# Front stage of a fused attention and mixture-of-experts kernel: work of the first four tiles spread between weight products, another load order, and bf16 products on TensorE during the first loads

## The chip, the cores and the metric

The kernel runs on one core of one Trainium2 chip. The metric is the device time of one execution in microseconds; the time before is the median of five runs. A profile of one further execution gives, for each engine, when each instruction ran and what it waited for. TensorE is called PE in the profile, its weight loads PEld, VectorE DVE, ScalarE ACT, GpSimd POOL, and SyncE, which here only issues transfers, SP.

## The reference

For hidden states `x` of 2 x 1024 tokens with 512 features, the reference computes a layer norm, single-head attention, a router-weighted mixture of two of eight experts, and a gate:

```python
xn = layernorm(x)                                   # mean and variance over 512, eps 1e-5
qkv = xn @ w_qkv.T + b_qkv                          # q, k, v of 512 each
s = softmax(q @ k.T / sqrt(512)) @ v @ w_out.T + b_out
logits = xn @ router_w + router_b                   # 8 experts, the best two, softmax of the two
h = silu(xn @ expert_w[e] + expert_b[e])            # combined with the two weights
y = xn + combined @ proj_w + proj_b
g = silu(norm_w * y / sqrt(mean(y * y) + 1e-6))
out = x + s * g
```

## The kernel before, in words

The 2048 tokens are 16 tiles of 128 rows. The kernel has a front stage, a stage of products per tile (`pv`), the router, the experts (`ph`), and attention with the projection and the gate. All arithmetic is float32, and the order of instructions on every engine is the order in which the Python code writes them (`keep_order`). A step that waits on an engine therefore holds everything written after it on the same engine. The same is true of the transfers that SP issues.

The change is in the front stage. What follows are its steps, with the names that the profile shows.

The matrices Wv and Wo are multiplied beforehand, so that one product of a tile gives values that already went through the output matrix. `load_wv(c)` brings a quarter of Wv (256 KB), `load_wo(n)` a half of Wo (512 KB), `spread` brings Wq in four transfers of 256 KB into `wZ`, in runs of 512 bytes, and `load_x(t)` brings a tile of `x` (256 KB). The router matrix is 16 KB and goes to columns of the tile `rwvo`, in runs of 32 bytes.

`turn_wv(c)` turns a quarter of Wv: four transpositions on PE against the identity into one bank of PSUM (`wvt`), and a copy by DVE (`wvT`). `product_vo(n, hc)` is one of eight weight products: four matmuls of 256 columns, which the profile lists as eight, since each float32 matmul is two passes, and a copy by ACT into `rwvo` (`pvo`, lines 363 to 374).

`norm(g)` treats two tiles. DVE computes mean and variance (`bnst`, `mv`), ACT a square root (`std`), DVE the reciprocal and the shift (`rstd`, `shift`), and ACT the scaled rows. For the first four tiles (`DIRECT = 4`) ACT makes the rows twice: as `xw`, which PE turns, and as `xn`, with columns in another order, which goes to DRAM for the experts. For the other tiles `xn` goes to DRAM (`put`) and comes back rearranged (`take`), and DVE turns it in blocks. `turn_x(t)` is that last step: for the first four tiles four PE transpositions into a bank (`xt`) and a DVE copy into `xnT`, for the others one DVE transposition of `xz`.

`turn_w` turns Wq on DVE (four instructions at line 134), `weighted` forms the sum `sq` from it on DVE (lines 285 and 287), and `columns` makes of it one column on PE (`pw`), which DVE copies into the router's columns of `rwvo`. `pbb` is a small product for a bias.

The loop over 16 tiles at line 403 then multiplies each turned tile by `rwvo` (`pv`, line 411): 265 columns, the router's nine among them, then 256. ACT copies the values (`vo`), DVE adds the router's bias (`lg`). Two double banks (`ps_big`) serve `pv`; four banks (`ps_mm`) serve all the small products in turn. In the loop, `norm` runs six tiles ahead of `pv`, and `turn_x` two tiles ahead.

Of the kernel before, what the change touches and what calls it, by code (L numbers as in the profile page):

```python
# [10 lines left out]
FP = mybir.dt.float32  # L11
BF = mybir.dt.bfloat16
I32 = mybir.dt.int32
AF = mybir.ActivationFunctionType
# [6 lines left out]
P = 128  # L21
# [6 lines left out]
def kernel(  # L28
# [17 lines left out]
    B, S, H = hidden.shape  # L46
    E = router_w.shape[1]
    KC = H // P
    NTOK = B * S
    NT = NTOK // P  # L50
# [7 lines left out]
    scale = 1.0 / math.sqrt(H)  # L58
# [103 lines left out]
    E1 = E + 1  # L162
# [7 lines left out]
    def load_x(t):  # L170
        x[t] = ln.tile([P, H], FP, tag="x", name=f"x{t}", bufs=8)
        sp.dma_start(x[t], x_d[:, t, :])
# [7 lines left out]
    def load_wv(c):  # L180
        sp.dma_start(wv_in[:, c, :], w_qkvT[ts(c, P), ts(2, H)])

    def load_wo(n):
        sp.dma_start(
            wo[:, :, ts(n, HH)], w_outT[:, ts(n, HH)].rearrange("(c p) h -> p c h", p=P)
        )

    act.dma_start(bqkv, b_qkv.rearrange("p (i c) -> p i c", i=3))
    act.dma_start(rw[:, :, 0:E], router_w.rearrange("(c p) e -> p c e", p=P))
    load_wv(0)  # L190
    load_wo(0)
    for c in range(1, KC):
        load_wv(c)
    for t in range(2):
        load_x(t)
    load_wo(1)
    spread(sp, wZ[0], w_qkvT[:, ts(0, H)])
    for t in range(2, 8):
        load_x(t)

    ident = const.tile([P, P], FP, name="ident")
    make_identity(nc, ident)
# [76 lines left out]
    def weighted(w_, bias, name):  # L279

        s_ = raw.tile([P, H], FP, tag="s", name=name, bufs=3)
        for c in range(KC):
            b_ = bias[:, c : c + 1]
            if c:
                dve.scalar_tensor_tensor(s_, w_[:, c, :], b_, s_, ALU.mult, ALU.add)
            else:
                dve.tensor_scalar(s_, w_[:, c, :], b_, None, ALU.mult)
        return s_

    def columns(s_, name):  # L290

        ps = ps_mm.tile([P, 512], FP, tag="mm", name=name)
        for c in range(KC):
            pe.matmul(
                ps[:, c : c + 1], lhsT=s_[:, ts(c, P)], rhs=ones[:, 0:1], start=True, stop=True
            )
        return ps[:, 0:KC]

    DIRECT = 4

    def norm(g):

        gs = ts(g, 2)
        two = (2 * g, 2 * g + 1)
        for t in two:
# [3 lines left out]
        act.activation(  # L309
            std[:, gs], mv[:, gs, 1:2].rearrange("p t o -> p (t o)"), AF.Sqrt, bias=ln_eps  # L310
        )
        dve.reciprocal(rstd[:, gs], std[:, gs])
        dve.scalar_tensor_tensor(
            shift[:, gs], mv[:, gs, 0:1].rearrange("p t o -> p (t o)"), -1.0, rstd[:, gs],
            ALU.mult, ALU.mult,
        )
        for t in two:
            scaled = dict(bias=shift[:, t : t + 1], scale=rstd[:, t : t + 1])
            if t < DIRECT:
                xw[t] = raw.tile([P, H], FP, tag="xw", name=f"xw{t}", bufs=DIRECT)  # L320
                act.activation(xw[t], x[t], AF.Identity, **scaled)
            xn_[t] = ln.tile([P, H], FP, tag="xn", name=f"xn{t}", bufs=5)
            act.activation(in_turn(xn_[t]), own(x[t]), AF.Identity, **scaled)
        if two[0] >= DIRECT:
            for t in two:
                xs[t] = dram.tile([4, P, P], FP, tag="xn_s", name=f"xn_s{t}", bufs=6)
                put(xs[t], xn_[t])
        for t in two:
            if t + 8 < NT:
                load_x(t + 8)  # L330
        for t in two:
            sp.dma_start(xn_d[ts(t, P), :], xn_[t])
        if two[0] >= DIRECT:
            for t in two:
                xz[t] = ln.tile([P, 4, P], FP, tag="xz", name=f"xz{t}", bufs=6)
                take(xz[t], xs.pop(t))

    xs, xz, xn_, xw = {}, {}, {}, {}

    def turn_x(t):  # L340
        dst = xnT[t // ST][:, :, ts(t % ST, P)]
        if t >= DIRECT:
            turn(dst, xz.pop(t))
            return
        ps = ps_mm.tile([P, 512], FP, tag="mm", name=f"xt{t}").rearrange(
            "p (j f) -> p j f", j=KC
        )
        for j in range(KC):
            pe.transpose(ps[:, j, :], xw[t][:, ts(j, P)], ident)
        dve.tensor_copy(dst, ps)  # L350
# [3 lines left out]
    def turn_wv(c):  # L354
        ps = ps_mm.tile([P, 512], FP, tag="mm", name=f"wvt{c}").rearrange(
            "p (o f) -> p o f", o=KC
        )
        for oc in range(KC):
            pe.transpose(ps[:, oc, :], wv_in[:, c, ts(oc, P)], ident)
        wvT[c] = raw.tile([P, KC, P], FP, name=f"wvT{c}")  # L360
        dve.tensor_copy(wvT[c], ps)

    def product_vo(n, hc):
        at_, size = halves[n]
        ps = ps_mm.tile([P, 512], FP, tag="mm", name=f"pvo{hc}_{n}")
        for c in range(KC):
            pe.matmul(
                ps[:, :size],
                lhsT=wvT[hc][:, c, :],
                rhs=wo[:, c, ts(n, HH)],  # L370
                start=(c == 0),
                stop=(c == KC - 1),
            )
        act.copy(rwvo[:, hc, at_ : at_ + size], ps[:, :size])
# [21 lines left out]
    pe.matmul(pbb[:, 0:KC], lhsT=ones, rhs=bb, start=True, stop=True)  # L396
    dve.tensor_reduce(rb[:, E:E1], pbb[:, 0:KC], AX.X, ALU.add)
    turn_x(0)
    turn_x(1)
    dve.tensor_copy(rw[:, :, E], columns(sq_, "pw"))  # L400


    for t in range(NT):
        if t % 2 == 0 and t + 6 < NT:
            norm(t // 2 + 3)
        if t + 2 < NT:
            turn_x(t + 2)
        pv = ps_big.tile([P, 2, 512], FP, tag="big", name=f"pv{t}")
        for n, cols in enumerate((ds(0, HH + E1), ds(HH + E1, HH))):
            for c in range(KC):  # L410
                pe.matmul(  # L411
                    pv[:, n, : HH + E1 * (1 - n)],
                    lhsT=xnT[t // ST][:, c, ts(t % ST, P)],
                    rhs=rwvo[:, c, cols],
                    start=(c == 0),
                    stop=(c == KC - 1),
                )
        dst = vo[t // ST][:, t % ST, :].rearrange("p (n f) -> p n f", n=2)
        act.copy(dst, pv[:, :, 0:HH])
        dve.tensor_tensor(lg1[:, t, :], pv[:, 0, HH : HH + E1], rb, ALU.add)  # L420
        if t == 1:
            spread(sp, wZ[1], w_qkvT[:, ts(1, H)])
        if t == 2:
            gps.dma_start(bo, b_out.partition_broadcast(P))
        if t == 4:
            turn_w(wqkT[:, KC:], wZ[1])
        if t == 6:
            sk_ = weighted(wqkT[:, KC:], bqk[:, 0], "sk")
        if t == 8:

            vb = weighted(wo, bqkv[:, 2], "vb")
        if t == 9:
            dve.tensor_copy(u, columns(sk_, "pu"))
        if t == 11:
            pvb = ps_mm.tile([P, 512], FP, tag="mm", name="pvb")
            pe.matmul(pvb, lhsT=ones, rhs=vb, start=True, stop=True)
            dve.tensor_tensor(bo, pvb, bo, ALU.add)
            close(raw_guard)
            ew_guard, ewp = pool("ew", side="right")
            ew = ewp.tile([P, E, KC, H], FP, name="ew")  # L440
        if t == 12:
            for e in range(E):
                sp.dma_start(ew[:, e], expert_w[e].rearrange("(c p) f -> p c f", p=P))
# [762 lines left out]
```

## Time and profile before

| | us |
|---|---|
| median of five runs | 558.38 |
| lowest and highest run | 552.31, 561.65 |
| all five | 552.75, 559.30, 561.65, 558.38, 552.31 |
| the profiled execution's own time | 554.18 |
| span from its first to its last instruction | 552.3 |
| PE busy, share of the span | 529.1, 96% |
| DVE busy, share | 314.5, 57% |
| ACT busy, share | 160.6, 29% |
| mean granted clock of PE | 0.986 |

The profiled execution took 554.18 us, of which 552.3 us lie between the first and the last instruction. The median of the runs is 4.20 us above it. A busy PE is not PE at its peak: a row for matmuls with the clock at half speed is as busy as one at full speed. The view of 40 slices therefore has a line of its own for the clock that PE was granted.

### The profile page before, as it was taken

Reading aid. Unit: us, or ns where it says so; the run is one execution under the profiler, and the core shown is the slowest. Engines: PE = TensorE matmul, PEld = TensorE weight load, DVE = VectorE, ACT = ScalarE, POOL = GpSimd, SP = SyncE. Lnnn points to the kernel's source line nnn. Section 1 sums busy time; section 2 is a strip of 40 time slices with the busy share of each in tenths; the row PEclk is TensorE's granted clock in tenths of the full one; section 3 lists DMA queues with packets and bytes.
Section 4 is the critical chain, followed back from the end, with each engine's and each line's share of the span. In section 5 each row is a group of like instructions: output and inputs, shape, how many; then the busy total and the mean of one; then the engine's idle time right before and its main releaser. Section 6 shows DMA issues by size and latency. Waiting matters only on the chain.

```text
span 552.3 us, 5745 instructions
## 1 busy us (share of the span) xinstructions
PE 529.1 (96%) x1736; PEld 323.4 (59%) x1736; DVE 314.5 (57%) x522; ACT 160.6 (29%) x262; POOL 224.8 (41%) x230
## 2 busy tenths in 40 slices
PE   5899999999999999999997999999999999999985
PEld 4788887444444444443545666756746556474855
DVE  1836763821333333343788257375798685948655
ACT  1634312111211111111323422423325243242413
POOL 5000000023245763220678536238837575646070
PEclk9979999999999999999997999999999999999999
DMA  9899569738899999989476913715416656282702
GB/s 249 257 328 270 178 201 381 290 98 262 262 279 329 301 313 293 290 248 278 157 223 205 331 54 110 271 39 193 188 38 183 237 162 256 88 293 78 266 31 83
DMA packets 90783, 118.65 MB, mean 215 GB/s; under 512 B 6912, under 2 KB 54912, under 8 KB 90624
## 3 DMA queue, kind: packets, MB, share of 16 engines
q1 hardware_dynamic: 78672, 89.15, 50.7%
q0 software_dynamic: 5792, 18.88, 10.9%
q10 hardware_dynamic: 6288, 10.25, 5.0%
q8 instruction: 14, 0.23, 0.2%
q14 instruction: 17, 0.14, 0.1%
HBM read 73.69 MB, written 44.56 MB: 214 GB/s over the span
## 4 chain that ended last, share of the span: by engine, by line
PE 63%; DMA 22%; DVE 7%; issue 5%; SPq 1%; ACT 1%; POOL 1%; ACTq 0%; DVEq 0%; POOLq 0%
PE so L1018 13%; PE pp L953 13%; PE pv L411 11%; PE po L891 10%; DMA xs<-xg 7%; DMA xg<-xn_d,tok 7%; PE pq L454 5%; PE pr L473 4%; PE ph L712 3%; PE pqk L485 2%; PE sc L934 1%; DMA ho_d<-h 1%; DMA sz<-xs 1%; DMA x<-_attn_hidden_states_dram 1%; DMA pz<-ps 1%
## 5 line engine op out<-in xcount | busy, mean ns | idle before, releaser
L712 PE MATMUL ph<-ew,gT 128*128 x280 | 120.6, 593 | 1.2 <-DVE gT L120 1.2
L686 POOL DMA_INDIRECT xg<-xn_d,tok x39 | 37.4, 959 | 183.2 <-DVE npast L632 103.9
L712 PEld LDWEIGHTS ph<-ew,gT 128*128 128x128 f32 x280 | 53.0, 190 | 68.6 <-issue 66.0
L738 DVE TENSOR_TENSOR h<-ph,eb 128x512 f32<-128x512 f32 x39 | 26.7, 687 | 74.3 <-issue 42.9
L411 PE MATMUL pv<-rwvo,xnT 128*128 128x265 f32 (+1 forms) x256 | 59.0, 391 | 0.0
L891 PE MATMUL po<-pw,ct 128*128 128x512 f32 x128 | 56.3, 593 | 2.1 <-DVE ct L120 2.1
L411 PEld LDWEIGHTS pv<-rwvo,xnT 128*128 128x128 f32 x256 | 49.3, 194 | 9.2 <-issue 0.5
L741 ACT ACTIVATE h<-h 128x512 f32<-128x512 f32 x39 | 24.6, 630 | 102.6 <-DVE h L738 82.4
L1025 DVE TENSOR_TENSOR o<-so,o 128x256 f32<-128x256 f32 (+1 forms) x57 | 22.9, 415 | 42.9 <-PE so L1018 21.4
L891 PEld LDWEIGHTS po<-pw,ct 128*128 128x128 f32 x128 | 24.2, 190 | 31.3 <-issue 31.2
L953 PE MATMUL pp<-xnT,qT 128*128 128x512 f32 x84 | 39.6, 593 | 0.4 <-DVE o L1025 0.4
L1052 POOL TENSOR_TENSOR o<-o,base 128x512 f32<-128x512 f32 x14 | 20.2, 1462 | 46.2 <-DVE o L1043 46.2
L1018 PE MATMUL so<-vo,pT 128*128 128x256 f32 x168 | 38.5, 379 | 0.0
L853 POOL DMA_INDIRECT hg<-ho_d,posi_m x32 | 30.9, 967 | 18.2 <-DMA cs<-hg 9.9
L120 DVE STREAM_TRANSPOSE gT<-sz 128x512 f32<-128x512 f32 x39 | 27.5, 705 | 19.0 <-DMA sz<-xs 18.9
L1018 PEld LDWEIGHTS so<-vo,pT 128*128 128x128 f32 x168 | 31.9, 190 | 7.3 <-issue 3.1
L921 ACT ACTIVATE pr<-sc,nm 128x1024 f32<-128x1024 f32 x16 | 18.3, 1142 | 60.3 <-DVE nm L918 60.3
L959 DVE TENSOR_TENSOR sc<-pp,sc 128x512 f32<-128x512 f32 x49 | 31.7, 682 | 6.6 <-PE pp L953 6.4
L473 PE MATMUL pr<-xnT,wqk 128*128 128x256 f32 x128 | 31.6, 408 | 3.0 <-DVE sc L959 3.0
L473 PEld LDWEIGHTS pr<-xnT,wqk 128*128 128x128 f32 x128 | 26.4, 207 | 9.3 <-DVE sc L959 3.4
L120 DVE STREAM_TRANSPOSE pT<-pz 128x1024 f32<-128x1024 f32 x14 | 28.3, 2019 | 0.0
L454 PE MATMUL pq<-xnT,wqk 128*128 128x512 f32 x64 | 28.1, 594 | 0.0
(198 smaller groups left out, 768.4 us busy)
## 6 DMA issues: line engine op xcount, KB each, us to landing
xs<-xg SPq DMA_DIRECT2D x39, 256.0 KB
sz<-xs SPq DMA_DIRECT2D x39, 256.0 KB
ho_d<-h ACTq DMA_DIRECT2D x39, 256.0 KB
ew<-in_L_ffn_expert_w_dram SPq DMA_DIRECT2D x8, 1024.0 KB
ps<-pr SPq DMA_DIRECT2D x16, 512.0 KB
pz<-ps SPq DMA_DIRECT2D x16, 512.0 KB
x<-_attn_hidden_states_dram SPq DMA_DIRECT2D x16, 256.0 KB
xn_d<-xn SPq DMA_DIRECT2D x16, 256.0 KB
```

What stands on the lines that cost most here:

```text
L120: dve.transpose(dst.rearrange(f"p j {order} -> p i j a", a=QP), z.rearrange("p i (j b) -> p i j b", b=QP),)
L411: pe.matmul(pv[:, n, : HH + E1 * (1 - n)], lhsT=xnT[t // ST][:, c, ts(t % ST, P)], rhs=rwvo[:, c, cols], start=(c == 0), stop=(c == KC - 1),)
L454: pe.matmul(ps[:, half, :], lhsT=wqk[:, c, ts(oc, P)], rhs=xnT[0][:, c, ts(half, 512)], start=(c == 0), stop=(c == KC - 1),)
L473: pe.matmul(ps[:, :PW], lhsT=wqk[:, c, ts(oc, P)], rhs=xnT[1][:, c, ts(k, PW)], start=(c == 0), stop=(c == KC - 1),)
L686: gps.indirect_dma_start(out=xg[s], out_offset=None, in_=xn_d, in_offset=bass.IndirectOffsetOnAxis(ap=tok[:, s : s + 1], axis=0),)
L712: pe.matmul(ph, lhsT=g_[:, c, :], rhs=ew[:, ds(r, 1), c, :].rearrange("p e f -> p (e f)"), start=(c == 0), stop=(c == KC - 1),)
L738: dve.tensor_tensor(h, ph, eb[:, ds(r, 1), :].rearrange("p e f -> p (e f)"), ALU.add)
L853: gps.indirect_dma_start(out=g_, out_offset=None, in_=ho_d, in_offset=bass.IndirectOffsetOnAxis(ap=posi_m[:, n, t : t + 1], axis=0),)
L891: pe.matmul(po, lhsT=c_[:, c, :], rhs=pw[:, c, :], start=(c == 0), stop=(c == KC - 1))
L953: pe.matmul(ps, lhsT=l_[:, c, :], rhs=r_[:, c, :], start=(c == 0), stop=(c == KH - 1))
L959: dve.tensor_tensor(dst, ps, other, ALU.add)
L1018: pe.matmul(ps[:, :w_], lhsT=l_[:, c, :], rhs=r_[:, c, :], start=(c == 0), stop=(c == SK - 1),)
```

## The change

The first transfers go in another order: two quarters of Wv ahead of Wo, four tiles of `x` ahead of the second half of Wo and of Wq, and the router matrix behind Wq on SP's queue, no longer on ACT's. A bf16 tile of ones is set by POOL ahead of the identity, and `hold(n)` issues n bf16 products of 256 columns into a bank that nobody reads: 12 ahead of `turn_wv(0)` and 6 ahead of `turn_wv(1)`.

`norm` is cut into `stats`, `shifts`, `direct` and `rows`, and for the first four tiles these pieces are written between the weight products. `turn_x(0)` and `turn_x(1)` stand ahead of `pbb`, the third group of `norm` stands behind the copy of `pw`, and `turn_x(2)` is the first step of the loop. In `pv` the 256 columns that hold no router column come first.

```diff
     act.dma_start(bqkv, b_qkv.rearrange("p (i c) -> p i c", i=3))
-    act.dma_start(rw[:, :, 0:E], router_w.rearrange("(c p) e -> p c e", p=P))
     load_wv(0)
+    load_wv(1)
     load_wo(0)
-    for c in range(1, KC):
+    for c in range(2, KC):
         load_wv(c)
-    for t in range(2):
+    for t in range(4):
         load_x(t)
     load_wo(1)
     spread(sp, wZ[0], w_qkvT[:, ts(0, H)])
-    for t in range(2, 8):
+    sp.dma_start(rw[:, :, 0:E], router_w.rearrange("(c p) e -> p c e", p=P))
+    for t in range(4, 8):
         load_x(t)
+    idle = const.tile([P, 2 * P], BF, name="idle")
+    gps.memset(idle, 1.0)
+
+    def hold(n):
+        ps = ps_mm.tile([P, 512], FP, tag="mm", name="hold")
+        for _ in range(n):
+            pe.matmul(ps[:, : 2 * P], lhsT=idle[:, 0:P], rhs=idle, start=True, stop=True)
...
+    def direct(t):
+        xw[t] = raw.tile([P, H], FP, tag="xw", name=f"xw{t}", bufs=DIRECT)
+        normed(xw[t], x[t], t)
...
+    def norm(g):
+        stats(g)
+        shifts(g)
+        rows(g)
...
+    hold(12)
     turn_wv(0)
+    hold(6)
     turn_wv(1)
-    for hc in range(KC):
-        product_vo(0, hc)
-        if hc + 2 < KC:
-            turn_wv(hc + 2)
-        if hc == 2:
-            norm(0)
+    product_vo(0, 0)
+    turn_wv(2)
+    stats(0)
+    product_vo(0, 1)
+    turn_wv(3)
+    product_vo(0, 2)
+    stats(1)
+    shifts(0)
+    direct(0)
+    product_vo(0, 3)
+    direct(1)
+    shifts(1)
     turn_w(wqkT[:, 0:KC], wZ[0])
     product_vo(1, 0)
-    norm(1)
+    direct(2)
+    direct(3)
 
     bb = raw.tile([P, KC], FP, name="bb")
     dve.tensor_tensor(bb, bqkv[:, 0, :], bqkv[:, 1, :], ALU.mult)
     product_vo(1, 1)
+    rows(0)
     sq_ = weighted(wqkT[:, 0:KC], bqk[:, 1], "sq")
     product_vo(1, 2)
-    norm(2)
+    turn_x(0)
     product_vo(1, 3)
+    rows(1)
+    turn_x(1)
     pbb = ps_mm.tile([P, 512], FP, tag="mm", name="pbb")
     pe.matmul(pbb[:, 0:KC], lhsT=ones, rhs=bb, start=True, stop=True)
     dve.tensor_reduce(rb[:, E:E1], pbb[:, 0:KC], AX.X, ALU.add)
-    turn_x(0)
-    turn_x(1)
     dve.tensor_copy(rw[:, :, E], columns(sq_, "pw"))
+    norm(2)
 
 
     for t in range(NT):
+        if t == 0:
+            turn_x(2)
         if t % 2 == 0 and t + 6 < NT:
             norm(t // 2 + 3)
-        if t + 2 < NT:
+        if 0 < t < NT - 2:
             turn_x(t + 2)
         pv = ps_big.tile([P, 2, 512], FP, tag="big", name=f"pv{t}")
-        for n, cols in enumerate((ds(0, HH + E1), ds(HH + E1, HH))):
+        for n, cols in ((1, ds(HH + E1, HH)), (0, ds(0, HH + E1))):
```

The new `stats`, `shifts` and `rows` hold the lines of the old `norm` unchanged: statistics and square root, reciprocal and shift, and the `xn` rows with their transfers (new loads of `x`, stores to `xn_d`, `put` and `take`).

More of the change, by code (lines that the diff above doesn't have):

```diff
@@ L299, with stats @@
     DIRECT = 4
-    def norm(g):
+    def stats(g):
         gs = ts(g, 2)
-        two = (2 * g, 2 * g + 1)
-        for t in two:
+        for t in (2 * g, 2 * g + 1):
             st = ln.tile([P, 6], FP, tag="bnst", name=f"bnst{t}", bufs=4)
@@ L311, in norm, with shifts @@
         )
+    def shifts(g):
+        gs = ts(g, 2)
         dve.reciprocal(rstd[:, gs], std[:, gs])
@@ L316, in norm, with normed, rows @@
         )
+    def normed(dst, src, t):
+        act.activation(
+            dst, src, AF.Identity, bias=shift[:, t : t + 1], scale=rstd[:, t : t + 1]
+        )
+    def direct(t):
+        xw[t] = raw.tile([P, H], FP, tag="xw", name=f"xw{t}", bufs=DIRECT)
+        normed(xw[t], x[t], t)
+    def rows(g):
+        two = (2 * g, 2 * g + 1)
         for t in two:
[L318 to L321, printed above, removed]
             xn_[t] = ln.tile([P, H], FP, tag="xn", name=f"xn{t}", bufs=5)
-            act.activation(in_turn(xn_[t]), own(x[t]), AF.Identity, **scaled)
+            normed(in_turn(xn_[t]), own(x[t]), t)
         if two[0] >= DIRECT:
```

## The prediction

> **What bounds the kernel now.** I read the page first, then PE by time, then the clock in slices of 1 us, then DVE and ACT over the same stretch, and SP's own waits last.
>
> ```profile
> span 552.3 us, 5745 instructions
> PE 529.1 (96%) x1736; PEld 323.4 (59%) x1736; DVE 314.5 (57%) x522; ACT 160.6 (29%) x262; POOL 224.8 (41%) x230
> ...
> PEclk9979999999999999999997999999999999999999
> ```
>
> PE is busy nearly throughout, so only a stage with holes or with a low clock has time to give. The clock line has two such places: the third slice (27.6 to 41.4 us) and the twenty-second. The change lies ahead of the first. PE's timeline there:
>
> ```profile
> 3.81 1.09 PE L359 MATMUL wvt<-ident,wv_in 128*128 128x128 f32 x4 [3.81 <-DMA wv_in<-in_L_attn_w_qkv_dram]
> 6.87 1.11 PE L359 MATMUL wvt<-ident,wv_in 128*128 128x128 f32 x4 [1.97 <-DMA wv_in<-in_L_attn_w_qkv_dram]
> 7.78 3.35 PE L367 MATMUL pvo<-wo,wvT 128*128 128x256 f32 x8
> ...
> 11.40 1.89 PE L367 MATMUL pvo<-wo,wvT 128*128 128x256 f32 x8
> 13.13 0.60 PE L359 MATMUL wvt<-ident,wv_in 128*128 128x128 f32 x4
> 13.57 10.53 PE L367 MATMUL pvo<-wo,wvT 128*128 128x256 f32 x48
> 23.93 0.28 PE L396 MATMUL pbb<-bb,ones 128*128 128x4 f32 x2
> 26.24 1.09 PE L349 MATMUL xt<-ident,xw 128*128 128x128 f32 x8 [2.03 <-ACT rwvo L374]
> 28.50 1.87 PE L294 MATMUL pw<-ones,sq 128*128 128x1 f32 x8 [1.16 <-DVE rb L397]
> 30.23 1.09 PE L349 MATMUL xt<-ident,xw 128*128 128x128 f32 x4
> 31.11 5.42 PE L411 MATMUL pv<-rwvo,xnT 128*128 128x265 f32 x16
> ```
>
> The weight products end at 24.1 us, but the first `pv` starts only at 31.11. Between them PE does little and waits twice, for ACT and for DVE. From there on `pv` is gapless, and the chain that ended last runs through PE's products down to the experts: what the front saves, the end should save. Eight rows of `pvo` take 10.53/6 = 1.755 us late, but 3.35 the first time: PE runs at half speed there. The 1 us slices show it happening again:
>
> ```profile
> 27.00:28.00 1.00, 0.34 (x4) 0.10 (x1) 0.61 (x2) 0.29 (x1) 0.00 (x0) 0.89 0.67 238
> 28.00:29.00 1.00, 0.50 (x3) 0.50 (x3) 0.96 (x5) 0.59 (x1) 0.00 (x0) 0.50 0.97 367
> ...
> 34.00:35.00 1.00, 1.00 (x4) 0.78 (x4) 0.00 (x0) 0.51 (x1) 0.00 (x0) 0.69 1.07 410
> ```
>
> The clock is the third number from the end. It falls at 27.78 (0.11 of a slice at a loss of 0.5 is 0.22 us) and returns at 34.62. DVE and ACT say what PE waited for:
>
> ```profile
> 18.17 2.49 DVE L134 STREAM_TRANSPOSE qT<-wZ 128x512 f32<-128x512 f32 x4
> ...
> 23.56 2.47 DVE L285 SCALAR_TENSOR_TENSOR sq<-qT,bqk,sq 128x512 f32<-128x512 f32 x3
> ...
> 28.36 1.28 DVE L350 COPY xnT<-xt 128x512 f32<-128x512 f32 x2
> ```
>
> ```profile
> 25.84 0.62 ACT L374 COPY rwvo<-pvo 128x256 f32<-128x256 f32 x2
> ```
>
> ACT copies the last weight products late, behind four `xw`/`xn` rows of 0.8 us, and `xt` waits 2.03 us for that bank. DVE ends `sq` at 26.03, works through the statistics of tiles 4 and 5, and only at 28.36 takes up what lets `pw` go. SP's waits tell when Wq lands:
>
> ```profile
> SPq L172 <- DMA wZ<-in_L_attn_w_qkv_dram: 2.2, 3, 1.1
> ```
>
> These end near 15.6 us. The slices show 180 to 207 GB/s from 11 to 16 us, the 512-byte runs of `wZ`, then 366. So `wZ` has landed by about 16.1, and `turn_w` at 18.17 did not wait for it; it waited behind `std` and `shift`.
>
> **The change, part by part.** First PE alone. The second quarter of Wv landed just before 6.87 with three 256 KB units and the router matrix ahead of it or beside it. Afterwards the same megabyte brings both quarters and half of Wo, so I let the first product start at 6.9 (7.78 before). Eight products by 1.755 are 14.0; `wvt` for the last two quarters and `xt` for two tiles are four by 0.44 (13.13 to 13.57), 1.8; `pbb` 0.3. That ends at 23.0. `pw` at full clock is 0.8 (1.87 here at half, and the same form in the loop at 68.64 lasts 0.79 in the chain) and `xt` for tile 2 is 0.44: `pv` could start at 24.2.
>
> Now DVE, which I think decides. `wZ` has two loads of `x` more ahead of it: 0.52 MB by some 350 GB/s (slices from 6 to 10 us, 313 to 397) is 1.5 us, so it lands at 17.6, less what the router matrix no longer takes (16 KB in 512 runs; nothing to 0.5 us). I take 17.5. All that stands ahead on DVE is done by then: `stats(0)` 10.0 to 11.8, the last `wvT`, `stats(1)` 12.5 to 14.2 by 1.69 a pair (14.38 to 16.07), the shifts by 15. Then `turn_w` 2.41 (18.17 to 20.58), `bb` and `sq` 3.07 (22.88 to 25.95), one copy of `xnT` 0.64: 23.6. The copy also frees `pw`'s bank. `pw` 0.8 and `xt` 0.44 give 24.85, later than PE's own 24.2. I take 24.9 for the first `pv`, against 31.11: 6.2 us.
>
> The second gain is the clock. The hole from 24.1 to 26.2 us and the thin work behind it brought the drop at 27.78. Its part in `pv` is 31.11 to 34.62, 3.5 us at half speed, or 1.75 us. Afterwards PE waits at most from 23.0 to 23.6. I count the 1.75 whole; bounds are nothing, if a hole stays, and 1.75.
>
> `hold`: `ph<-ident` at line 730 has this form, six in 0.82 us of which the last is 0.27, so 0.11 each at full clock and 0.22 at half. Twelve are 2.6 us from 1.05 (POOL sets `ident` in 0.20 us at 0.81; `idle` takes that place), to 3.7: before the first quarter is there at 3.81. Six from 4.9 reach 6.2 at half speed; `wvt` for the second quarter then ends by 7.2, at worst 0.3 us late on PE, which has 0.65 to spare. If `hold` keeps the clock up, the first product saves 3.35 - 1.755 = 1.6 us; if not, PE's 24.2 becomes 25.8, and `pv` starts 0.9 later than I say. Its cover is DVE's chain, so I put `hold` at nothing and keep 0 to 0.9 as a loss.
>
> The clock's own row agrees with a window: fall and return are 6.84 us apart, two times 3.42. The Trainium skill (TensorE: Matmul & The Clock Gate, Part 1) states a free-running window of 3413 ns after which a busy PE is let go; the same page (Part 4: PE-mode transpose) says that transpositions do not count as busy in the same way, which speaks against this change, since `wvt` stands between the two `hold`s. By that rule the first product could run cold and the sum lose the 0.9 us; no run here shows it yet.
>
> ACT: `std` with its table load (1.28) now stands ahead of the copies of `pvo` 1 and 2, and holds the copy of the second to 13.4. Its bank is next written at about 15, so it costs nothing; with 1.6 us less cover PE would wait. The eight rows of four tiles are the same instructions, spread out.
>
> The `pv` loop: DVE turns to `stats(2)` only after `pw`, at 25.0 (25.95 before). So `shift` for tiles 4, 5 is ready at 27.4, and for 6, 7 at 30.45; ACT makes `xn` for 6 and 7 by 31.9 and only then copies the first `vo`, to 32.5. The third `pv` needs that double bank, with `lg`, at 32.75; PE arrives at 24.9 + 3.51 + 0.44 + 3.51 = 32.4 to 32.6. I charge 0.15. The halves' order lets the first 256 columns run without `pw`'s copy; that copy is done at 24.6 anyway, so nothing.
>
> SP: `put` of tile 4 follows `xn`, about 1 us earlier than 29.25; `take` some 31.7 (32.77 before), while tile 4 is wanted by PE at 39.7, not 47.5. Landing is not shown. From SP's own wait between `put` and `take` of tile 6 (35.14 to 38.70) a trip is 3.6 us: 35.8 and turned by 37.1, in time. The other bound is DVE's start before, 43.56, one us earlier: 42.5, turned at 43.6, and 3.9 us are given back. I take the trip, the nearest row.
>
> Sum: 6.2 + 1.75 - 0.15 = 7.8 us. The profiled execution goes from 554.18 to 546.4. The measured runs are two close to it or below and three 4.2 to 7.5 us above, and PE's rows in one profile cannot say why. I take the middle of all six executions, (554.18 + 558.38)/2 = 556.3, and predict 548.5.
>
> **The rivals.** *Wq comes late.* The SP queue and 512-byte runs speak for it; that SP is not held by any buffer there speaks against. If `wZ` lands at 20, `pv` starts at 27.4, and PE stands idle from 23.0 to 26.1, more than the hole that lowered the clock before. Then the 1.75 is lost too: 31.11 - 27.4 = 3.7 us, 552.6.
>
> *The trip through DRAM decides.* The DMA share is 0.93 to 1.15 from 34 to 42 us, which speaks for it; the 3.6 us trip against. By the bound above, 7.8 - 3.9 = 3.9 us, 552.4.
>
> *`hold` does not raise the clock.* The 0.9 us above: 549.4. This is the case that the change does not do what it says, and it hides inside the forecast.
>
> *Slower.* One mechanism: DVE's order puts `sq`, both `xnT` copies, `rb` and `pw` behind `turn_w`, so that all PE work waits for `wZ` alone. From a landing at 31.11 - 7.4 = 23.7 it is slower than before, since the clock falls as before. At 30, with `wZ` at half its rate and held by the queue, `pv` starts at 37.4: 6.3 us later, 562.6. The five us of the transfer in the slices speak against.
>
> **How the numbers follow.** Forecast (with `hold`'s failure in it) 0.66, late Wq 0.15, the trip 0.11, slower 0.08. A measurement of this kernel can tell about 1% from no change, 5.6 us. The forecast is above it, the two middle rivals within: faster 0.66, same 0.26, slower 0.08. The range takes the lower execution, 552.3 - 7.8 = 544.5, less 1.5 for the second low clock: it falls near 297.8 and is back by 304.5, about 3.4 us lost, and where the windows fall against PE's 3.0 us hole there is chance. So 543. Upward it takes in both middle rivals with 2.5 us for the spread of the runs: 555.
>
> **What would show it.** `pv` starts at 24.9 with 8 rows in 1.76 us and no fall of the clock until it; the first `pvo` takes 1.8 us; `turn_w` starts at about 17.5 and waits for `wZ`; the third `pv` starts at 32.8; `pv` ends near 84 (91.9 before). If `pv` starts before 27 but the fourth or later tile waits for `xz`, the trip was right. If PE waits over 2 us ahead of `pw`, Wq was late. If `pv` ends 7.8 us early and the time does not follow, a later stage was not bound by PE and my reading of it was wrong.

## The result, and the profile after

The kernel after the change has a median of 555.88 us over 42 executions (551.12 to 559.27), the kernel before, run beside it, 554.07 us over 79 (545.32 to 562.52): by the medians 0.3% more. The ratios given here are taken over each kernel's fast executions, those at most 1.5% above its fastest, and by the times these are all 42 of after but only 36 of the 79 of before. The ratio is 1.0098 with a 95% interval of 1.0078 to 1.0118: the change made the kernel about 1% slower. Forecast were 548.5 us and a gain. The profiled execution after took 556.13 us, with a span of 554.4.

The page of the kernel after, in the lines that were shown of before:

```profile
span 554.4 us, 5785 instructions
PE 531.2 (96%) x1754; PEld 321.0 (58%) x1754; DVE 316.8 (57%) x522; ACT 160.2 (29%) x262; POOL 225.1 (41%) x231
...
PEclk9999999999999999999999999999999999999989
```

The low clock in the third slice is gone, and so is the second one near 298 us; a new one stands at the end. PE's timeline of the front:

```profile
1.18 2.74 PE L209 MATMUL hold<-idle 128*128 128x256 bf16 x12 [1.18 <-POOL idle L204]
...
7.29 1.96 PE L392 MATMUL pvo<-wo,wvT 128*128 128x256 f32 x8 [0.80 <-DVE wvT L386]
...
25.43 1.02 PE L304 MATMUL pw<-ones,sq 128*128 128x1 f32 x8 [2.23 <-DVE sq L295]
26.32 1.08 PE L374 MATMUL xt<-ident,xw 128*128 128x128 f32 x4
27.19 4.95 PE L449 MATMUL pv<-rwvo,xnT 128*128 128x256 f32 x16
```

The first weight product takes 1.96 us (3.35 before). Its half speed in before is read from that duration alone: the granted clock reads 1.00 in the slices of both kernels from 7 to 11 us. But `pw` waits 2.23 us for `sq`, and the first `pv` starts at 27.19, not at 24.9. It takes 4.95 us, where a run below at full clock takes 3.76. Slices of 1 us, with the granted clock as the third number from the end:

```profile
26.00:27.00 1.00, 1.00 (x9) 1.00 (x9) 1.00 (x4) 0.00 (x0) 0.00 (x0) 0.68 0.82 244
...
29.00:30.00 1.00, 1.00 (x5) 0.79 (x4) 1.00 (x2) 0.97 (x2) 0.00 (x0) 0.62 0.01 2
```

The clock falls at about 26.3 and is back at about 29.75, one stretch of 3.4 us where before had two. DVE says why `sq` is late:

```profile
19.61 2.49 DVE L134 STREAM_TRANSPOSE qT<-wZ 128x512 f32<-128x512 f32 x4 [4.67 <-DMA wZ<-in_L_attn_w_qkv_dram]
...
22.82 2.47 DVE L295 SCALAR_TENSOR_TENSOR sq<-qT,bqk,sq 128x512 f32<-128x512 f32 x3
```

DVE stands idle for 4.67 us until Wq lands, 2.1 us later than I said. That is the rival "Wq comes late", and it leaves 2.8 us of gain where `pqk` starts (88.92, before 91.70). Those 2.8 us still ought to show at the end. Instead, between `ph` and `sc`, the experts took 129.8 us (132.24 to 262.04) where before took 122.9 (135.01 to 257.90). The groups of the experts' product and of the transposition that feeds it, before and then after (behind the second bar: idle time of the engine just before them, and what ended most of it):

```profile
L712 PE MATMUL ph<-ew,gT 128*128 x280 | 120.6, 593 | 1.2 <-DVE gT L120 1.2
L120 DVE STREAM_TRANSPOSE gT<-sz 128x512 f32<-128x512 f32 x39 | 27.5, 705 | 19.0 <-DMA sz<-xs 18.9
```

```profile
L750 PE MATMUL ph<-ew,gT 128*128 x280 | 123.1, 596 | 4.8 <-DVE gT L120 3.4
L120 DVE STREAM_TRANSPOSE gT<-sz 128x512 f32<-128x512 f32 x39 | 27.7, 709 | 52.8 <-DMA sz<-xs 52.7
```

PE now waits for `gT`, `gT` for `sz`, and `sz` is the last step of a loop on which nothing was changed. For each slot of 128 gathered rows POOL gathers them (`xg`, three buffers), SP puts them into DRAM (`xs`) and takes them back in another order (`sz`), DVE turns them (`gT`), PE multiplies.

The whole account of the two profiles: `ph` starts 2.8 us earlier, the experts take 6.9 more, from `sc` to `po` it takes 4.6 less (42.2, before 46.8; before had the clock at half speed for about 6.8 us there, where 16 rows of `pr` took 6.73 us instead of 3.72), and the rest takes 2.6 more, with a 3.0 us wait for `ct` (2.1 in before) and a low clock near 530 us. Together +2.1 us, the difference of the spans. Before's profiled execution, 554.18 us, is longer than any of the 36 that the ratio is taken over, so this account explains the difference of two executions and not the 1%.

### The profile page after: what moved, and what is told of

Read it like the earlier page. It is cut to its first block, busy times and chain, and to the rows that moved or that the text cites. A ratio compares the mean times of both kernels' runs of the same rounds, so it can differ in the third digit from the quotient of the medians.

```text
span 554.4 us, 5785 instructions
## 1 busy us (share of the span) xinstructions
PE 531.2 (96%) x1754; PEld 321.0 (58%) x1754; DVE 316.8 (57%) x522; ACT 160.2 (29%) x262; POOL 225.1 (41%) x231
## 3 DMA queue, kind: packets, MB, share of 16 engines
q0 software_dynamic: 5792, 18.88, 11.5%
## 4 chain that ended last, share of the span: by engine, by line
PE 58%; DMA 27%; DVE 6%; issue 5%; ACT 1%; SPq 1%; POOL 0%; DVEq 0%; ACTq 0%; POOLq 0%
PE so L1056 13%; PE pp L991 13%; PE po L929 10%; DMA xs<-xg 9%; PE pv L449 8%; DMA xg<-xn_d,tok 7%; PE pq L492 5%; PE pr L511 3%; PE pqk L523 2%; PE ph L750 2%; DMA wZ<-in_L_attn_w_qkv_dram 2%; DMA ho_d<-h 2%; DMA pz<-ps 1%; DMA xn_s<-xn 1%; DMA wv_in<-in_L_attn_w_qkv_dram 1%
## 5 line engine op out<-in xcount | busy, mean ns | idle before, releaser
L750 PE MATMUL ph<-ew,gT 128*128 x280 | 123.1, 596 | 4.8 <-DVE gT L120 3.4
L929 PE MATMUL po<-pw,ct 128*128 128x512 f32 x128 | 58.0, 607 | 3.0 <-DVE ct L120 3.0
L449 PE MATMUL pv<-rwvo,xnT 128*128 128x256 f32 (+1 forms) x256 | 59.3, 390 | 0.8 <-DVE lg L458 0.8
L449 PEld LDWEIGHTS pv<-rwvo,xnT 128*128 128x128 f32 x256 | 48.8, 193 | 10.7 <-DVE lg L458 2.1
L776 DVE TENSOR_TENSOR h<-ph,eb 128x512 f32<-128x512 f32 x39 | 26.6, 683 | 46.1 <-PE ph L750 30.4
L511 PE MATMUL pr<-xnT,wqk 128*128 128x256 f32 x128 | 28.5, 380 | 2.4 <-DVE sc L997 2.4
L511 PEld LDWEIGHTS pr<-xnT,wqk 128*128 128x128 f32 x128 | 24.2, 190 | 7.7 <-DVE sc L997 2.8
```

Of the source, the lines that this page charges most:

```text
L449: pe.matmul(pv[:, n, : HH + E1 * (1 - n)], lhsT=xnT[t // ST][:, c, ts(t % ST, P)], rhs=rwvo[:, c, cols], start=(c == 0), stop=(c == KC - 1),)
L511: pe.matmul(ps[:, :PW], lhsT=wqk[:, c, ts(oc, P)], rhs=xnT[1][:, c, ts(k, PW)], start=(c == 0), stop=(c == KC - 1),)
L750: pe.matmul(ph, lhsT=g_[:, c, :], rhs=ew[:, ds(r, 1), c, :].rearrange("p e f -> p (e f)"), start=(c == 0), stop=(c == KC - 1),)
L776: dve.tensor_tensor(h, ph, eb[:, ds(r, 1), :].rearrange("p e f -> p (e f)"), ALU.add)
L929: pe.matmul(po, lhsT=c_[:, c, :], rhs=pw[:, c, :], start=(c == 0), stop=(c == KC - 1))
```

## The experiments

Each kernel ran beside the kernel before on one chip, both kernels of a pair on the same one; kernels that are no pair can have run on different chips. Names starting with b are edits of the kernel before, with a of the kernel after. The table holds, from each one's profile, the starts of the first `pv`, `pqk` and `ph`, the time from `ph` to `sc` and from `sc` to `po`, and the ratio to before. One profile stands for each kernel: a_pwend's is of its shortest execution (544.85 us of 544.85 to 553.12), those of before, b_pad (554.71 us) and a_pw (555.87 us) are of long ones.

| kernel | pv | pqk | ph | ph to sc | sc to po | ratio, 95% interval |
|---|---|---|---|---|---|---|
| before | 31.11 | 91.70 | 135.01 | 122.9 | 46.8 | 1 |
| after | 27.19 | 88.92 | 132.24 | 129.8 | 42.2 | 1.0098 [1.0078, 1.0118] |
| b_notrip | 30.16 | 90.49 | 133.80 | 121.4 | 44.8 | 0.9998 [0.9966, 1.0031] |
| a_notrip | 26.74 | 89.00 | 132.32 | 121.4 | 44.8 | 0.9987 [0.9947, 1.0027] |
| b_xg4 | 30.44 | 90.85 | 134.16 | 121.4 | 40.5 | 0.9899 [0.9844, 0.9954] |
| a_xg4 | 27.32 | 89.21 | 132.52 | 121.4 | 40.5 | 0.9878 [0.9818, 0.9937] |
| a_xg4_nohold | 27.86 | 90.07 | 133.38 | 121.4 | 40.5 | 0.9891 [0.9843, 0.9938] |
| a_again | 28.69 | 90.77 | 134.09 | 127.9 | 44.0 | 1.0117 [1.0087, 1.0147] |
| a_ones | 27.64 | 89.37 | 132.68 | 127.6 | 46.1 | 1.0085 [1.0047, 1.0123] |
| b_pad | 30.97 | 91.67 | 134.98 | 125.5 | 44.9 | 0.9989 [0.9948, 1.0030] |
| a_pw | 30.64 | 92.70 | 136.02 | 126.2 | 42.7 | none |
| b_pw | 30.18 | 90.53 | 133.85 | 129.9 | 43.1 | 1.0147 [1.0096, 1.0198] |
| a_pwend | 26.25 | 88.45 | 131.76 | 121.4 | 42.7 | 1.0001 [0.9966, 1.0037] |
| b_pwend | 30.48 | 91.07 | 134.39 | 121.4 | 42.8 | 1.0002 [0.9966, 1.0039] |
| a_xg4_x2 | 24.28 | 91.88 | 135.19 | 121.4 | 40.5 | 0.9974 [0.9938, 1.0011] |
| a_xg4_xt | 23.15 | 91.27 | 134.59 | 121.4 | 40.5 | 0.9947 [0.9916, 0.9977] |
| a_xg4_xt2 | 25.32 | 91.88 | 135.20 | 121.4 | 40.5 | 0.9908 [0.9870, 0.9945] |
| a_xg4_xt2_pwend | 24.66 | 91.20 | 134.52 | 121.4 | 44.4 | 0.9967 [0.9933, 1.0001] |

**Is it the loop of the gathered rows?** The pair without the trip through DRAM:

```diff
-        turn(gT[s], sz.pop(s), "(i a)")
+        turn(gT[s], xg.pop(s).rearrange("p (i f) -> p i f", i=4), "(i a)")
...
-    steps = ((gather, 4), (put_s, 3), (take_s, 2), (turn_s, 1), (expert, 0))
+    steps = ((gather, 3), (turn_s, 1), (expert, 0))
```

b_notrip:

> The kernel before, with the experts' trip through DRAM left out: DVE turns the gathered rows themselves, so put and take of each slot are gone (the experts get rows in a wrong order). Theory L, the loop of gather, put and take sets the experts' pace: the stage shrinks from 122.7 us to about 35 x 3.44 = 120 to 121 us and PE waits for no gT. Theory P, PE sets the pace: the same 120 to 121 us, since it was already near it. Alone it tells little; it is the partner of the same cut in the changed kernel.

a_notrip:

> The changed kernel with the same trip left out. Theory L: the front's saving of 2.8 us (first pqk at 88.92 instead of 91.70) now reaches the end, so this is 2 to 4 us faster than its partner, and the experts last 120 to 121 us instead of 129.8. Rival N, the change harms a later stage by itself (addresses, phases of the clock, attention): this is as slow as its partner or slower, although its front is 2.8 us shorter.

And the pair with a fourth buffer; the room comes from a constant of which only 40 columns are used, and in a_xg4 `hold` reads a tile that is there anyway:

```diff
-    iota = const.tile([P, P], FP, name="iota")
+    iota = const.tile([P, NSP], FP, name="iota")
...
-        xg[s] = mo.tile([P, H], FP, tag="xg", name=f"xg{s}")
+        xg[s] = mo.tile([P, H], FP, tag="xg", name=f"xg{s}", bufs=4)
```

b_xg4:

> The kernel before with four buffers for gathered rows instead of three (and a constant cut from 128 to 40 columns to make room). Theory L, the loop of gather and put over three buffers is latency-bound at 3.6 us a slot: the loop gets a third more room, the experts go from 122.7 to 120 to 122 us, the time falls by 1 to 4 us. Rival B, the DMA engines' bandwidth is the bound: no change within 1 us, since the same bytes move.

a_xg4:

> The changed kernel with four buffers for gathered rows (same constant cut; the tile of ones serves hold). Theory L: the experts go from 129.8 to 120 to 123 us, the time falls by 5 to 8 us, and it is 2 to 4 us faster than the kernel before with four buffers. Rival B: within 2 us of the changed kernel, the experts still 127 us or more.

In all four the experts take 121.4 us, PE's own pace, with the short front as with the long one. The kernel behind the change is then 0.1% (without the trip) and 0.2% (four buffers) ahead of the other, 0.6 and 1.2 us by the ratios, and the intervals of each pair overlap. Theory L had said 2 to 4 us for both pairs: the pace came as it said, that gain did not. So the loss of 1% comes from this loop. The chain that ended last tells the same story, and told it before the change. Its shares by engine and by line, of before, of after and of a_xg4:

```profile
PE 63%; DMA 22%; DVE 7%; issue 5%; SPq 1%; ACT 1%; POOL 1%; ACTq 0%; DVEq 0%; POOLq 0%
PE so L1018 13%; PE pp L953 13%; PE pv L411 11%; PE po L891 10%; DMA xs<-xg 7%; DMA xg<-xn_d,tok 7%; PE pq L454 5%; PE pr L473 4%; PE ph L712 3%; PE pqk L485 2%; PE sc L934 1%; DMA ho_d<-h 1%; DMA sz<-xs 1%; DMA x<-_attn_hidden_states_dram 1%; DMA pz<-ps 1%
```

```profile
PE 58%; DMA 27%; DVE 6%; issue 5%; ACT 1%; SPq 1%; POOL 0%; DVEq 0%; ACTq 0%; POOLq 0%
PE so L1056 13%; PE pp L991 13%; PE po L929 10%; DMA xs<-xg 9%; PE pv L449 8%; DMA xg<-xn_d,tok 7%; PE pq L492 5%; PE pr L511 3%; PE pqk L523 2%; PE ph L750 2%; DMA wZ<-in_L_attn_w_qkv_dram 2%; DMA ho_d<-h 2%; DMA pz<-ps 1%; DMA xn_s<-xn 1%
```

```profile
PE 82%; DVE 8%; DMA 5%; issue 3%; ACT 1%; SPq 1%; DVEq 0%
PE ph L749 20%; PE so L1055 15%; PE pp L990 13%; PE po L928 10%; PE pv L448 8%; PE pq L491 5%; PE pr L510 3%; PE sc L971 3%; PE pqk L522 3%; DMA xn_s<-xn 2%; DMA wZ<-in_L_attn_w_qkv_dram 2%; DMA wv_in<-in_L_attn_w_qkv_dram 1%; DVE y L945 1%; DVE tw L853 1%; DVE sc L996 1%
```

`ph` is busy for 120.6 us of before's span, 22%, and has 3% of its chain; `xs` and `xg`, transfers of the loop, have 14%. With four buffers `ph` has 20% and the loop's transfers are gone from the list.

**Is it only where the tiles lie?** The tile of ones that `hold` reads shifts the tiles behind it in memory. a_again is the kernel after once more; a_ones lets `hold` read an existing tile, so that nothing shifts; b_pad puts the idle tile into the kernel before.

a_again:

> The changed kernel once more, beside the kernel before on one chip. Theory L, the experts' loop over three buffers takes what the front saves and its pace varies from run to run: the two medians lie within 3 us, and the profile shows experts that last 121 to 130 us with PE waiting for gT. Rival A, the new tile of ones moves all later tiles by 512 bytes a partition and slows their transfers: this is 2 us or more slower, with experts of 128 us or more each time.

a_ones:

> The changed kernel with hold reading the tile of ones that the kernel has anyway, so no tile is added and all addresses are as before. Theory L: like the changed kernel within 1.5 us. Rival A: 3 us or more faster than the changed kernel, and 1 to 3 us faster than the kernel before.

```diff
-    idle = const.tile([P, 2 * P], BF, name="idle")
-    gps.memset(idle, 1.0)
+    idle = ones.bitcast(BF)
```

b_pad:

> The kernel before with only the new tile added and set by POOL, never read. Theory L: like the kernel before within 1.5 us. Rival A: 3 us or more slower than the kernel before.

a_again lies 5.9 us above before by the medians (554.67 and 548.73), where theory L had said at most 3: the loss is regular. But the addresses are not it: a_ones is as slow as the change (1.0085) and b_pad as fast as before (0.9989).

**Is it the load of `proj_w`?** The starts of the gathers, counted from the first, agree between before and after until the fifteenth (44.7 and 44.3 us). In between SP issues the four 256 KB loads of `proj_w`. The sixteenth gather then comes 8.8 us after the fifteenth in before, 12.1 in after, 11.5 and 12.2 in a_again and a_ones. POOL's timeline in after, from that gather on:

```profile
169.29 0.97 POOL L724 DMA_INDIRECT xg<-xn_d,tok  x1 [9.80 <-DMA xs<-xg]
171.72 0.96 POOL L724 DMA_INDIRECT xg<-xn_d,tok  x1 [0.16 <-issue]
174.13 0.97 POOL L724 DMA_INDIRECT xg<-xn_d,tok  x1 [0.16 <-issue]
179.95 0.97 POOL L724 DMA_INDIRECT xg<-xn_d,tok  x1 [3.54 <-DMA xs<-xg]
182.38 0.96 POOL L724 DMA_INDIRECT xg<-xn_d,tok  x1 [0.16 <-issue]
184.79 0.96 POOL L724 DMA_INDIRECT xg<-xn_d,tok  x1 [0.16 <-issue]
190.94 0.96 POOL L724 DMA_INDIRECT xg<-xn_d,tok  x1 [3.88 <-DMA xs<-xg]
```

After one wait of 9.80 us the gathers go in threes, the next two sets of buffers 10.7 and 11.0 us later, 3.55 and 3.66 us a slot, where PE needs at most 121.4/35 = 3.47 for each of its 35 products. The first trial moved the loads ahead of the loop:

```diff
+    for q in range(4):
+        sp.dma_start(
+            pw[ts(q, QP)], proj_w[ts(q, P), :].rearrange("(j b) f -> b j f", b=QP)
+        )
...
-        if s == LR:
-            for q in range(4):
-                sp.dma_start(
-                    pw[ts(q, QP)], proj_w[ts(q, P), :].rearrange("(j b) f -> b j f", b=QP)
-                )
```

a_pw:

> The kernel after the change, with three buffers for the gathered rows, but the four loads of `proj_w` issued ahead of the experts instead of at the ninth slot. Theory W (the 1 MB of `proj_w` in the midst of the experts holds the gathers once, 8.8 us before the change and 11.5 to 12.2 us behind it, and after that hold the gathers run in bunches of three, 3.7 us a slot): without the load the gathers keep the pace of the products, the experts take at most 123 us as in before (127.6 to 129.8 in the three runs behind the change), and the time is 3 to 6 us under the after kernel's 555, that is 549 to 552. Rival L (the loop of gather, put, take over three buffers loses its pace by itself, whatever is loaded): the bunching comes anyway, the experts stay at 127 us or more and the time within 1.5 us of 555.

b_pw:

> The kernel before the change with the same edit: the four loads of `proj_w` ahead of the experts. Theory W: the hold of 8.8 us goes, the experts take some 121 to 122 us as with four buffers or without the trip, and the time falls by 1 to 4 us; then the kernel behind the change with the same edit is 1 to 2 us faster than this one, since its front is that much shorter. Rival L: no difference beyond 1 us from before.

Theory W got this wrong. b_pw became 1.5% slower than before; of a_pw's six executions one took 543.40 us and five 552.20 to 555.87, so that no ratio is given. The megabyte had only found another gather to hold: the fourth came at 12.3 us in a_pw and at 13.4 in b_pw, instead of 7.9 in before. From there on a_pw's gathers came in bunches to the end, (139.9 - 12.3)/35 = 3.65 us each. A hold at either place put the three buffers in step, and the loop did not find back in these profiles. a_pw's execution of 543.40 us, as short as those with four buffers, has no profile; it suggests that the loop does not lose its pace every time. The second trial took the loads out of the loop:

```diff
-        if s == LR:
-            for q in range(4):
-                sp.dma_start(
-                    pw[ts(q, QP)], proj_w[ts(q, P), :].rearrange("(j b) f -> b j f", b=QP)
-                )
+    for q in range(4):
+        sp.dma_start(
+            pw[ts(q, QP)], proj_w[ts(q, P), :].rearrange("(j b) f -> b j f", b=QP)
+        )
     close(mo_guard)
```

a_pwend:

> The kernel after the change with three buffers, the loads of `proj_w` moved behind the experts' loop (`po`, which needs them, starts some 42 us later). Moving them ahead of the loop did not remove the bunches: the 1 MB then held the fourth gather, at 12.3 us instead of 8, and the gathers ran at 3.68 us a slot from there. Theory P (a hold of the gathers, wherever it comes, sets the three buffers in step and the loop keeps the bunched pace; without a hold it keeps the products' pace): the gathers go on at 3.2 to 3.4 us a slot, from `ph` to `sc` it takes 121.5 to 123 us instead of 127.6 to 129.8, and the time is 545 to 548. Rival L (three buffers lose the pace without any hold): 126 us or more from `ph` to `sc`, time 552 or more.

b_pwend:

> The kernel before the change with the loads of `proj_w` behind the experts' loop. Theory P: as in the pair, 121.5 to 123 us from `ph` to `sc`, time 546.5 to 550, and the kernel behind the change with the same edit is 1 to 2.5 us faster, since its shorter front is no longer lost. Rival L: 125 us or more from `ph` to `sc`, and the time spreads from 545 to 560 as that of before.

The experts take 121.4 us in both, with three buffers and the trip in place. Waits of POOL, DVE and PE from 130 to 253 us, in after and then in a_pwend (total, times, longest):

```profile
POOL xg L724 <- DMA xs<-xg: 74.1, 23, 9.8
DVE gT L120 <- DMA sz<-xs: 36.8, 21, 2.8
PEld ph L750 <- DVE gT L120: 12.0, 14, 1.8
PE ph L750 <- DVE gT L120: 3.4, 7, 0.9
```

```profile
POOL xg L724 <- DMA xs<-xg: 61.7, 27, 4.7
POOL xg L724 <- issue: 2.6, 6, 0.7
```

Without the loads the longest wait of a gather is 4.7 us, and neither `gT` nor `ph` waits for the loop. b_pwend's 549.6 us lie within what was expected, a_pwend's 549.4 miss their 545 to 548, and the pair shows no difference (1.0001 and 1.0002), where 1 to 2.5 us had been expected, although `ph` starts 2.6 us earlier behind the change. So removing the hold takes away the change's 1%, and the front's gain stays below what the runs can tell.

The same runs say something of the kernel before. Its executions went from 545.6 to 560.8 us beside b_pwend (547.0 to 551.7), and from 545.9 to 561.4 beside b_notrip (548.5 to 551.3) and b_xg4 (543.6 to 546.0): what takes the loop's hold away takes away the long executions too. In b_pad's profile, of a long execution, the sixteenth gather comes 9.9 us after the fifteenth, and the gathers soon go in threes. So the kernel before seems to lose the pace in part of its executions and the kernel after in most: 20 of the 79 executions of before were shorter than the shortest of the 42 of after. This is argued from the times and one profile, not shown.

**What is the front worth when nothing eats it?** With four buffers I varied the front. a_xg4_nohold leaves out `hold(12)` and `hold(6)`:

> The changed kernel with four buffers, without the bf16 products of hold. My prediction put hold at nothing, covered by DVE's chain behind Wq: then the first pvo takes 3.3 us instead of 1.8 us, pw still starts when DVE lets it, at 25.4 to 26.0, and the time is within 1 us of the changed kernel with four buffers (543.43). Rival: hold carries the front's gain; then pv starts 1.5 us later and the time is 545 or more.

Its first weight product takes 3.75 us:

```profile
7.49 3.75 PE L391 MATMUL pvo<-wo,wvT 128*128 128x256 f32 x8 [1.81 <-DMA wo<-in_L_attn_w_out_dram]
```

With `hold` it took 1.96. Yet the first `pv` moves only from 27.32 to 27.86, and DVE took up Wq 0.55 us later in this profile (20.68 instead of 20.13), which is as much. The ratio to before goes from 0.9878 to 0.9891: `hold` raises the clock, and Wq's lateness covers what it gains. The Trainium skill (TensorE: Matmul & The Clock Gate, Part 4: PE-mode transpose) says that transpositions do not count as busy in the same way. The run without `hold` agrees as far as it goes: eight transpositions ahead of this product left the product at half speed, though a wait of 1.81 us stands there too. The wait alone did not do it: a_xg4, with `hold`, has four transpositions and a wait of 1.91 us at the same place.

```profile
7.43 1.96 PE L391 MATMUL pvo<-wo,wvT 128*128 128x256 f32 x8 [1.91 <-DMA wo<-in_L_attn_w_out_dram]
```

a_xg4_x2 loads only two tiles of `x` ahead of Wq, as before, with the work on the other two moved behind `sq`:

```diff
-    for t in range(4):
+    for t in range(2):
         load_x(t)
     load_wo(1)
     spread(sp, wZ[0], w_qkvT[:, ts(0, H)])
     sp.dma_start(rw[:, :, 0:E], router_w.rearrange("(c p) e -> p c e", p=P))
-    for t in range(4, 8):
+    for t in range(2, 8):
         load_x(t)
```

> The kernel after the change with four buffers (543.4 us earlier), and the load order of x as before: only x0 and x1 ahead of Wo's second half and Wq, x2 and x3 behind; the statistics and scaled rows of tiles 2 and 3 move behind the chain of Wq. Theory Q (Wq's landing is late because half a megabyte was put ahead of it): 512 KB at the 390 GB/s seen at 7 to 10 us take 1.3 us, so DVE's first transposition of Wq starts at 18.3 to 18.9 instead of 19.6 to 20.1, the first `pv` at about 26, and the time is 0.8 to 1.5 us lower. Rival R (Wq's own short runs at 180 to 210 GB/s share the engines with whatever is queued behind it, so the order ahead of it does not set its landing): the transposition starts at 19.6 or later and the time does not fall.

DVE took up Wq at 17.57 instead of 20.13, which is 2.6 us for half a megabyte (1.5 to 4.7 against the seven landings listed at the end). PE hardly waited ahead of `pv`, and the clock held:

```profile
23.39 1.02 PE L303 MATMUL pw<-ones,sq 128*128 128x1 f32 x8 [0.29 <-DVE sq L294]
24.28 3.76 PE L448 MATMUL pv<-rwvo,xnT 128*128 128x256 f32 x16
...
36.32 17.82 PE L448 MATMUL pv<-rwvo,xnT 128*128 128x256 f32 x80 [3.59 <-DVE xnT L374]
56.68 3.56 PE L448 MATMUL pv<-rwvo,xnT 128*128 128x256 f32 x15 [2.54 <-DVE lg L457]
```

The front that I had predicted is here, and it brings nothing: PE waits 3.59 us for a turned tile, the third, whose load and work this edit moved back, then 2.54 us for `lg`, and `pqk` starts at 91.88, later than in a_xg4. The clock reads 1.00 from 30 to 40 us, around the wait of 3.59 us, so a wait of that length need not lower it. The theory had the landing right, even undersized, and the time wrong. a_xg4_xt fills the wait for Wq instead, with the first halves of two `pv`:

```diff
-    turn_w(wqkT[:, 0:KC], wZ[0])
     product_vo(1, 0)
...
+    turn_x(0)
...
+    turn_x(1)
     product_vo(1, 2)
+    turn_w(wqkT[:, 0:KC], wZ[0])
...
+    pv_half(0, 1)
+    pv_half(1, 1)
+    dve.tensor_copy(rw[:, :, E], columns(sq_, "pw"))
```

> The kernel after the change with four buffers (543.4 us earlier), and the work that does not need Wq ahead of the wait for it: the transpositions of x0 and x1 stand ahead of the transposition of Wq on DVE, and the halves of the first two `pv` that need no column of Wq run while DVE weighs Wq; the fifth and sixth tile's statistics start earlier. Theory Q: PE's idle time from about 23.5 to 27.3 is filled with 16 products (2 tiles, about 2.4 us at full clock or 4.9 at half), so the stage `pv` ends 2.5 to 4 us earlier, `pqk` starts at 85.5 to 87 instead of 89.2, and with the experts keeping pace the time is 540 to 541.5. Rival S (a later wait, for the second Wq at the fifth tile or for x's rows, takes the gain): `pqk` starts at 88.5 or later and the time is within 1 us of 543.4.

Rival S was right. The first `pv` starts at 23.15, and DVE then stands at the second Wq, with `lg` queued behind it and PE behind `lg`:

```profile
51.34 2.49 DVE L134 STREAM_TRANSPOSE qT<-wZ 128x512 f32<-128x512 f32 x4 [5.57 <-DMA wZ<-in_L_attn_w_qkv_dram]
```

a_xg4_xt2 moves that transposition two tiles back (`if t == 4:` becomes `if t == 6:`, and the weighing goes from 6 to 7):

> The kernel with four buffers whose first `pv` starts at 23.15, but with the transposition of the second Wq at the seventh tile instead of the fifth, and its weighing at the eighth. There DVE had waited 5.57 us for the second Wq, from 45.77 to 51.34, PE stood 3.91 us behind it and ran at half clock afterwards. Theory Q (that wait alone took the front's gain): `pqk` starts at 85 to 87 instead of 91.27, and the time is 540 to 542 instead of 545.4 (four buffers without that reordering: 543.4). Rival S (the next wait, for x's rows or the accumulators, takes it): `pqk` at 88.5 or later, time 543 or more.

The wait only moved on, to the rows that come back from DRAM. DVE's waits from 25 to 92 us:

```profile
DVE xnT L120 <- DMA xz<-xn_s: 5.7, 3, 3.8
```

From 40 to 65 us the DMA engines have a busy share of 1.01 to 1.18 in each slice of 5 us, at 236 to 333 GB/s. In this stage every tile from the fifth on is loaded, put, taken and written for the gathers, 1 MB a tile. The four kernels that start `pv` at 23.2 to 25.3 reach `pqk` at 91.2 to 91.9, and those that start it at 26.3 to 27.9 reach it at 88.5 to 90.1.

a_xg4_xt2_pwend adds the late loads of `proj_w`:

> The last kernel with the loads of `proj_w` behind the experts as well. With four buffers the experts already take 121.4 us, the products' own time, so theory P expects no change beyond 0.5 us, or a gain of that size if the outputs of the experts, which share the DMA engines with the loads, land earlier. Rival: the loads now collide with the collection of the experts' rows at 255 to 290 and `po` starts 1 us or more later, and the time is 1 us longer.

Its rival was right: `po` starts at 300.28 instead of 297.09, and the ratio is 0.6% worse. Behind the loop the loads meet the collection of the experts' rows (44.4 us from `sc` to `po` in place of 40.5). a_pwend and b_pwend take 42.7 and 42.8 us there, but a_pw, whose loads are early, takes 42.7 as well, so it is not shown what keeps that pair from the times of four buffers. The lowest ratio of the study is a_xg4's, 1.2% below before; those of a_xg4_nohold, b_xg4 and a_xg4_xt2 lie within its interval.

## Why the prediction was wrong, step by step

- **The base.** 556.3 us were assumed for the kernel before; beside the change it had 554.07. From there a gain of 7.8 us would have meant 546.3, so the gain was missed by 9.6 us, more than 548.5 against 555.88 shows.
- **Products of the front.** The first weight product was said to start at 6.9 and take 1.8 us; it started at 7.29 and took 1.96. Right. `hold` at nothing, with up to 0.9 to lose: without it `pv` came 0.54 us later, and Wq 0.55. Right, since the cover was there.
- **DVE decides.** Right: `pw` waited 2.23 us for `sq`.
- **Wq lands at 17.5: mis-sized.** It landed at 19.61. I read the end of the transfer (16.1) from the slice in which the rate went up again, and added 1.5 us for half a megabyte at 350 GB/s. a_xg4_x2 speaks for both terms being short: with only two tiles ahead Wq is there at 17.57 in its one profile, and the other two cost 2.6 us. The first `pv` came 2.3 us later than said for that reason.
- **The clock is kept.** Wrong in consequence. The 2.23 us wait brought one drop of 3.4 us in place of two. Where that wait was gone (a_xg4_x2) the drop was gone, as the step says. But a later wait of 3.59 us in a_xg4_x2 brought no drop, so the runs give no length from which a wait lowers the clock.
- **`pv` is gapless: only just true.** After the change it lost 0.8 us. But the two middle rivals that I gave 0.15 and 0.11 are not alternatives, they lie one behind the other: had Wq come at 17.5, the second Wq and the trip through DRAM would likely have taken the 3 us. a_xg4_xt, where PE stood 3.91 us behind the second Wq, and a_xg4_xt2, where the turned rows came late, speak for that. None of the four kernels with an early `pv` came near the forecast of 84 for its end.
- **"What the front saves, the end should save": the step that failed.** It stands on my reading of the chain, that it runs through PE's products down to the experts. The page's chain said otherwise, in a line that I did not weigh: `ph` has 22% of the span and 3% of the chain. In that execution the experts ran near the pace of PE only because the loop of the gathers kept up with it, and a hold that was 3.3 us longer, at the load of `proj_w`, went with a loss of 6.9 us.
- **The slower case** had 0.08, on a Wq as late as 23.7. The kernel became slower by another mechanism, outside the range that I had looked at.

Shown: the loss lies in the loop over three buffers (four buffers, or no trip, remove it), and the loads of `proj_w` inside it set it off (in the profiles without them it does not occur). Not shown: why that hold is 11.5 to 12.2 us behind the change and 8.8 to 9.9 in before and b_pad, and why the gathers went in threes after the 9.9 of b_pad and not at once after the 8.8 of before. SP issues the same transfers there in the same order; it took 4.15 us for the four issues in after but 2.27 in a_again, 2.38 in before and 2.36 in b_pad, so the issue isn't it. How the transfers fall against each other in time may be it; no run tested that. Open as well is how much of the front's 1.5 to 2.6 us reaches the end: the three pairs with an undisturbed loop say 0.0, 0.6 and 1.2 us, with intervals of some 2 to 3 us to either side.

## What to carry to other kernels

Before a saving is carried to the end of a kernel, compare each later stage's share of the chain with its share of the span: a product with 22% of the span and 3% of the chain was fed just in time by something else here, and passed on nothing. Where a kernel's times spread, look whether a loop in it keeps its pace only in some executions, and compare all of them before a change is judged by the best. A loop over a few buffers that only just keeps pace should be given one buffer more before anything around it is tuned, and a large load should not be put into its midst. And rivals that lie one behind the other add up: when the first wait is removed, price the second before you count the gain.

## What the runs showed of the hardware

- A load of 1 MB beside a loop of gathers held one gather for 9.8 us, and the loop of three buffers then ran in threes, at first 3.55 to 3.66 us a slot. With four buffers (a_xg4) one was held 9.1 us and PE did not wait.
- Transfers in runs of 512 bytes moved 166 to 209 GB/s while Wq came in (12 to 18 us in after), against 297 to 404 for those ahead of it with longer runs (3 to 11 us). The Trainium skill (DMA: Bandwidth & Descriptors, Specifications) gives 512 bytes as the size from which a transfer reaches line rate; these rates do not agree. Each of the slow transfers also fills only 32 partitions, and no run separates that from the length of the runs.
- With the same front the landing of Wq varied from profile to profile: DVE took it up at 19.06, 19.56, 19.61, 19.71, 20.13, 21.51 and 22.22 us. One profile says little about a landing to better than 2 us.
